# First attention: the norm of 512 tokens made alone, that of the other 1536 together; both batches prepared beside the first group's maxima; values cleared on ScalarE

## The chip, the cores and the metric

The kernel runs on one core of a Trainium2 chip. The metric is the device time of one execution in microseconds (us); lower is better. The profile is of one execution on that core, and its times count from the first instruction. Engines: TensorE (PE; its weight loads are PEld), VectorE (DVE), ScalarE (ACT), GpSimd (POOL) and SyncE (SP), which in this kernel issues the DMAs.

## The reference

Two layers of attention and experts over x of shape (2, 1024, 128), each `x = x + block(norm(x))`. The change lies in the first block:

```python
x = x + _L0_attn_ref(_layernorm(x, axis=-1), ...)

def _L0_attn_ref(x, ln_scale, ln_bias, wq, wk, wv):
    xn = _layernorm(x, ln_scale, ln_bias)
    q, k, v = (xn @ w, in 16 heads of 8, for w in wq, wk, wv)
    scores = einsum('bhid,bhjd->bhij', q, k)
    probs = softmax(scores / sqrt(128))
    return einsum('bhij,bhjd->bhid', probs, v) + xn
```

The outer norm and the norm inside the block are one norm in the kernel (L233 and L237), with scale and bias applied after the transposes. After this block come 8 experts (two chosen per token, and a shared one), a causal attention with 8 heads, and 16 experts.

## The kernel before, in words

The 2048 tokens are four chunks of 512 (`x_0` to `x_3`); two chunks are one batch item. Everything the change touches is in `attn0` and the helpers it calls.

Preparing a chunk has these pieces. `stats` (L129) takes mean and variance of four tiles of 128 tokens on VectorE. `rsqrt` (L117) makes the factors by Newton steps of small VectorE operations. L244 or L248 writes the normalised `xn`. TensorE transposes it (L167), scale and bias make `xT` (L270, L272 or, in `prep_x0`, a function that before never calls, L259 and L260), and `split` (L156) writes a rounded high part on ScalarE and the residual on VectorE or POOL (L159). `prep_k` and `prep_q` multiply by the weights in three passes (`mm3`, L163), split the result into two halves `hl0` and `hl1` (two buffers for each), store it in three DMAs of 256 KB (L304) into a scratch tensor in DRAM, and load it from there in the layout that the score matmuls want (`bands`, L308): 768 KB for k and q of the first group's chunks, 1 MB for others. The scratch tensors also hold rows of ones (L212, L221). `banded` (L294) makes the block of head group 0 directly, without DRAM. `prep_v` copies v into `V`, whose other columns are cleared at L224 and L225. `prep_res` (L328) adds the normalised x to the residual on POOL.

The attention itself runs over 16 groups n: a chunk of 512 queries and 4 heads each. For each group there are two streams. The score stream `s_unit` (L353) makes, for 128 queries, 512 keys and 2 heads, two matmuls (L363) and one VectorE maximum over them (L368): 16 units a group. After the last, `s_finish` (L376) writes the negated maxima into `mexp` (L379) and, four steps later, `row` makes `QX` (L387, L389, and L391 on ScalarE), the queries with the maximum as one more row. The second stream, `st_unit` (L398), makes transposed scores for 128 keys, one head and 512 queries (L407), ScalarE takes the exponential (L413), and `av_half` (L420) multiplies by V (L427): 32 units a group. `av_finish` and `av_add` (L439, L444) divide by the sum and add to x.

The order of TensorE is written out by hand (L506, `manual_schedule`); the order of the other engines and of the DMA queue is planned at build time by a simulated time line, with `issue_after` as fixed orders between two instructions of one engine, and is not changed at run time. A lead of 38 steps (L507) runs half a score unit a step, so 19 units, which are group 0 and three units of group 1. At step 1 and every fourth step it runs one piece of `side` (k of chunk 0, k of chunk 1, q of chunk 0, v of both) and some warming matmuls on ones (L374), whose result is not used. The main loop (L521) then runs one `st_unit` and half a score unit a step, so one group in 32 steps. There q of chunk 1 and the residuals come first, and from step 16 `prep((2, 3))` prepares the second batch item, one piece every fourth step, with two warming matmuls beside each between steps 16 and 54 (L532). The experts' weights of the first layer are loaded in the prologue (`ffn0_weights`, L219). Scores against QM and KS of other chunks are needed from group 4 (queries of chunk 1) and group 8 (second batch item).

Of the kernel before, what the change touches and what calls it, by code (L numbers as in the profile page):

```python
# [10 lines left out]
F32 = mybir.dt.float32  # L11
# [10 lines left out]
B = 2  # L22
# [50 lines left out]
class Net:  # L73
# [13 lines left out]
    def setup(self, ctx):  # L87
# [21 lines left out]
        nc.vector.memset(ones, 1.0)  # L109
        self.ones_r = self.const.tile([128, 128], F32R, name="ones_r")  # L110
# [6 lines left out]
    def rsqrt(self, v, n, name):  # L117
        nc = self.nc
        y = self.small.tile([128, n], F32, tag="rsy", name=f"rs_{name}")
        w = self.small.tile([128, n], F32, tag="rsw", name=f"rw_{name}")  # L120
# [8 lines left out]
    def stats(self, srcs, name):  # L129
        nc = self.nc  # L130
        n = len(srcs)
        st = self.small.tile([128, n, nc.vector.BN_STATS_DIM], F32, tag="bnst", name=f"bs_{name}", bufs=2)
# [23 lines left out]
    def split(self, dst, src, lo=None):  # L156
        nc = self.nc
        nc.scalar.copy(dst[0], src)  # L158
        (lo or nc.vector).tensor_sub(dst[1], src, dst[0].bitcast(F32))  # L159

# [8 lines left out]
    def attn0(self, ctx, cb, side_plan):  # L169
# [22 lines left out]
        ld = nc.sync.dma_start  # L192
        ld(out=wq0[0], in_=a["a0wq0"])
# [6 lines left out]
        ld(out=lnsb, in_=a["a0ln"].partition_broadcast(128))  # L200
# [10 lines left out]
        for c, k in list(scratch)[:3]:  # L211
            nc.sync.dma_start(out=scratch[c, k][:, :, 24:32, :], in_=self.hot_r.bitcast(F32))  # L212
        for x in mexp:
            nc.gpsimd.tensor_scalar_mul(x, self.ones.rearrange("p (t r) -> p t r", t=TPC), 0.0)
        nc.gpsimd.tensor_copy(id_r[0], self.ident)
        nc.gpsimd.tensor_scalar_mul(id_r[1], self.ident, hm[:, 4:5])
        self.load_x(2)
        self.load_x(3)
        self.ffn0_weights()  # L219
        for c, k in list(scratch)[3:]:  # L220
            nc.sync.dma_start(out=scratch[c, k][:, :, 24:32, :], in_=self.hot_r.bitcast(F32))  # L221
        for b in range(B):
            for i in range(2):
                nc.gpsimd.memset(V[b][i], 0.0)  # L224
                nc.gpsimd.memset(V[b][i][:, :, :, 8:9], 1.0)  # L225
        xns, xTs = {}, {}

        def prep_ln(cs, act=()):
            n = TPC * len(cs)
            src = [self.x[c][:, t, :] for c in cs for t in range(TPC)]  # L230
            mv = yield from self.stats(src, f"a0_{cs[0]}")
# [3 lines left out]
            if act:  # L235
                nm = self.small.tile([128, n], F32, tag="rsn", name=f"rn_a0_{cs[0]}")
                nc.vector.scalar_tensor_tensor(nm, mv[:, :, 0], -1.0, rs, ALU.mult, ALU.mult)  # L237
            yield
            for i, c in enumerate(cs):
                xn = xns[c] = self.tok.tile([128, TPC, D], F32, tag="xn", name=f"xn0_{c}")  # L240
                for t in range(TPC):
# [9 lines left out]
                    if t % 2 == 1:  # L251
                        yield
# [1027 lines left out]
```

## Time and profile before

| | us |
|---|---|
| three runs | 931.33, 937.6, 937.7 (median 937.6) |
| the profiled execution | 938.26 |
| its span, first to last instruction | 936.5 |
| first maximum of group 0 (L368) starts | 20.75 |
| last maximum of group 0 done (L379) | 45.76 |
| first transposed score (L407) | 48.06 |
| L379 of groups 1, 2, 3, 4, 5, 6 | 67.19, 93.89, 123.78, 144.30, 165.25, 184.81 |
| mean granted TensorE clock | 0.974 of full |

A row of the profile that ends in a bracket tells how long the engine was idle just before, and what released it. A row of the chain of waits is start, duration, and what ran; a row of a stage table is the stretch, its length, the busy time of PE, PEld, DVE, ACT and POOL with the number of instructions, the granted clock, the busy share of the 16 DMA engines and GB/s. A row of SyncE's waits has the total, the number and the longest.

### The profile page before, as it was taken

The page shows a single profiled execution, that of the slowest core. Times are in us where ns is not written, and L with a number is a line of the kernel's source. Part 1 is how long each engine was busy: PE and PEld are TensorE (multiplying, and loading weights), DVE is VectorE, ACT ScalarE, POOL GpSimd, SP SyncE. Part 2 cuts the span into 40 slices and gives each one's busy share as a digit, 9 for nine tenths or more (in the row PEclk, how much of TensorE's full clock was granted, in tenths as well). Part 3 has the DMA queues.
Part 4 walks back from the last instruction along what each step waited for, and adds up shares of the span by engine and source line. Part 5 has one row for each costly group of instructions (what it writes and reads, how often), then busy time and mean ns, then how long its engine had stood idle before and what let it go on. Part 6 is the DMA issues. An engine that isn't in the chain of part 4 may idle for free.

```text
span 936.5 us, 17186 instructions
## 1 busy us (share of the span) xinstructions
PE 889.5 (95%) x6469; PEld 602.9 (64%) x6469; DVE 800.3 (85%) x1636; ACT 597.9 (64%) x1153; POOL 315.7 (34%) x397
## 2 busy tenths in 40 slices
PE   7999899999999999989799998999999899998997
PEld 4543344444444443458688997988889799866775
DVE  7897789999999999358787788899979797799986
ACT  3178788998898898655344555445445355478775
POOL 9001300000010000023664757375737274236332
PEclk9999999999999999699999999999999999999999
DMA  6620440011000000023000001000000000064462
GB/s 181 203 79 1 149 145 1 1 46 57 13 27 10 1 1 2 2 95 100 13 9 4 12 21 49 1 24 1 2 2 24 2 25 12 24 192 152 143 199 70
DMA packets 32044, 49.13 MB, mean 52 GB/s; under 512 B 4544, under 2 KB 10488, under 8 KB 31960
## 3 DMA queue, kind: packets, MB, share of 16 engines
q1 hardware_dynamic: 31960, 48.03, 16.1%
q8 instruction: 51, 0.84, 0.4%
q14 instruction: 33, 0.27, 0.1%
HBM read 38.36 MB, written 9.65 MB: 51 GB/s over the span
## 4 chain that ended last, share of the span: by engine, by line
PE 66%; DVE 17%; ACT 7%; issue 5%; DMA 2%; POOL 1%; SPq 0%; DVEq 0%; ACTq 0%; POOLq 0%
PE av L427 14%; PE st L407 11%; PE o L905 10%; PE st L872 9%; ACT pt L413 3%; PE s L833 3%; DVE mx L368 2%; DVE f1f L1091 2%; PE vp L163 2%; PE hot L374 2%; PE qp L163 2%; PE st L879 2%; PE f0y L695 2%; DVE s L842 1%; PE stw L407 1%
## 5 line engine op out<-in xcount | busy, mean ns | idle before, releaser
L368 DVE TENSOR_REDUCE mx<-s 128x2 f32<-128x1024 f32 x256 | 299.7, 1219 | 21.6 <-PE s L363 18.3
L413 ACT ACTIVATE pt<-st 128x512 f32<-128x512 f32 x476 | 252.9, 602 | 32.7 <-PE s L363 21.2
L427 PE MATMUL av<-pt,V 128*32 128x256 f32 x2048 | 166.5, 405 | 0.0
L905 PE MATMUL o<-V,pt 128*128 128x129 f32 x1152 | 156.0, 276 | 1.5 <-ACT pt L884 0.7
L363 PE MATMUL s<-KS,QM 24*128 24x512 f32 x512 | 152.4, 499 | 3.0 <-DVE mx L368 2.1
L905 PEld LDWEIGHTS o<-V,pt 128*128 128x128 f32 x1152 | 148.7, 191 | 9.9 <-ACT pt L884 1.0
L407 PE MATMUL st<-QX,KS 25*128 25x512 f32 x476 | 144.8, 498 | 6.1 <-ACT pt L413 4.1
L872 PE MATMUL st<-Q,K 128*128 128x512 f32 (+1 forms) x480 | 136.6, 393 | 5.3 <-DVE rB_q L776 2.5
L407 PEld LDWEIGHTS st<-QX,KS 25*128 25x128 f32 x476 | 63.1, 182 | 101.4 <-ACT pt L413 47.2
L456 POOL TENSOR_TENSOR x<-x,ov 128x128 f32<-128x128 f32 x16 | 7.3, 454 | 322.4 <-DVE ov L453 322.4
L872 PEld LDWEIGHTS st<-Q,K 128*128 128x128 f32 x480 | 80.1, 191 | 16.9 <-DVE rB_q L776 3.7
L884 ACT ACTIVATE pt<-st 128x512 f32<-128x512 f32 x88 | 47.7, 544 | 59.6 <-PE st L879 51.8
L427 PEld LDWEIGHTS av<-pt,V 128*32 128x32 f32 x2048 | 42.9, 110 | 64.5 <-issue 61.1
L884 ACT ACTIVATE pt<-pt 128x512 f32<-128x512 f32 x72 | 43.2, 603 | 48.6 <-DVE pt L882 48.3
L363 PEld LDWEIGHTS s<-KS,QM 24*128 24x128 f32 x512 | 65.6, 183 | 11.4 <-DVE mx L368 7.9
L918 POOL TENSOR_TENSOR x<-x,w 128x128 f32<-128x128 f32 x128 | 59.3, 463 | 26.4 <-ACT w L916 22.0
L833 PE MATMUL s<-K,Q 128*128 128x512 f32 (+2 forms) x192 | 62.6, 357 | 0.8 <-DVE m L842 0.7
L163 PE MATMUL f1y<-f1s,f1w 128*128 128x512 f32 x192 | 56.3, 413 | 5.5 <-POOL f1s L159 3.1
L916 ACT ACTIVATE w<-o,rz 128x128 f32<-128x128 f32 x128 | 39.9, 364 | 33.4 <-DVE rz L912 29.0
L159 POOL TENSOR_TENSOR f1s<-f1f,f1s 128x512 fp32r<-128x512 f32 x24 | 36.2, 1510 | 59.6 <-ACT f1s L158 57.1
L1091 DVE SCALAR_TENSOR_TENSOR f1f<-f1f,f1gb 128x512 f32<-128x512 f32 x64 | 49.9, 797 | 7.4 <-ACT f1f L1090 6.6
L888 POOL TENSOR_SCALAR_AFFINE_SELECT pt<-pt 128x256 f32<-128x256 f32 x64 | 26.4, 415 | 86.8 <-ACT pt L884 86.6
(231 smaller groups left out, 1585.8 us busy)
## 6 DMA issues: line engine op xcount, KB each, us to landing
f1gb<-f1gd SPq DMA_DIRECT2D x64, 256.0 KB
f0gb<-f0gd SPq DMA_DIRECT2D x32, 128.0 KB
kd<-k SPq DMA_DIRECT2D x12, 256.0 KB
qd<-q SPq DMA_DIRECT2D x12, 256.0 KB
QM<-qd SPq DMA_DIRECT2D x3, 1024.0 KB
mb<-md SPq DMA_DIRECT2D x10, 256.0 KB
KS<-kd SPq DMA_DIRECT2D x2, 1024.0 KB
KS<-kd SPq DMA_DIRECT2D x2, 768.0 KB
```

The source lines that it names most:

```text
L163: self.nc.tensor.matmul(out, lhsT=lhs[l], rhs=rhs[r], start=start and i == 0, stop=stop and i == 2)
L363: self.last_s = nc.tensor.matmul(ps[:, k, :], lhsT=QM[c][r, g, cols(t)], rhs=KS[c // 2][r, g, cols(h, CH)], start=True, stop=True)
L368: self.marks["V"] = nc.vector.tensor_reduce(mxs[n][:, h, 2 * pr : 2 * pr + 2, t : t + 1], ps, AX.X, ALU.max, negate=True)
L407: nc.tensor.matmul(ps, lhsT=KS[c // 2][32 * j : 32 * j + 25, g, cols(kt)], rhs=QX[n][32 * j : 32 * j + 25, :], start=True, stop=True,)
L413: self.marks["A"] = nc.scalar.activation(e, ps, AF.Exp, scale=INV_SQRT_D)
L427: return nc.tensor.matmul(avs[n][cols(j, 32), q], lhsT=V[c // 2][kt // 4][:, kt % 4, 4 * g + j, :], rhs=es[j][:, q], start=kt == 0 and i = ...
L833: nc.tensor.matmul(s[:, 0 : k1 - k0], lhsT=Q[0][:, h, cols(qt)], rhs=K[0][:, k0:k1], start=True, stop=True)
L872: k = nc.tensor.matmul(o, lhsT=K[l][:, cols(kt)], rhs=Q[r][:, :, q0 : q0 + w], start=i == 0, stop=apart and i == 2)
L884: k = nc.scalar.activation(e[:, :, 256 - w :], o, AF.Exp, scale=INV_SQRT_D)
L905: nc.tensor.matmul(acc[t][:, h, :], lhsT=e[:, h, cols(t)], rhs=V[:, kt, h, :], start=(kt == 0 and h == 0), stop=(kt == qt and h == 1),)
L918: nc.gpsimd.tensor_add(xt, xt, w[:, h, :])
L1091: nc.vector.scalar_tensor_tensor(f, f, F7, gbs[e], ALU.min, ALU.mult)
```

## The change

Only chunk 0's norm is made ahead of the streams, by `prep_x0`; the statistics of chunks 1 to 3 go into VectorE's order behind chunk 0's `xn` and its split, and their factors are computed in one set of small operations of width 12 behind the first `banded` blocks. The lead's plan is a table by step: it now holds all of k, q and v of all four chunks, chunk 1's direct block at step 10, the last five rows of ones at step 5, and the residuals. The loads from DRAM (L308) are put off by three steps behind their stores, and are ordered on SyncE behind the last store issued so far. The order of group 0's score units becomes keys 0 to 511 for all queries, then keys 512 to 1023. In the main loop the second item's preparation and the warming matmuls of L532 go; the first experts' weights are loaded at step 24. `V` of the first item and `mexp` are cleared by ScalarE copies of a zero; `V` of the second item stays on POOL. x of chunks 2 and 3 is loaded ahead of the scratch rows. Two small buffers become single. The marks "L" and "D", which the cut diff mostly leaves out, name the last ScalarE piece and the last store, behind which later pieces are ordered.

```diff
+        self.zero = self.const.tile([128, 1], F32, name="zero")
+        nc.vector.memset(self.zero, 0.0)
...
-        w = self.small.tile([128, n], F32, tag="rsw", name=f"rw_{name}")
+        w = self.small.tile([128, n], F32, tag="rsw", name=f"rw_{name}", bufs=1)
...
-        st = self.small.tile([128, n, nc.vector.BN_STATS_DIM], F32, tag="bnst", name=f"bs_{name}", bufs=2)
+        st = self.small.tile([128, n, nc.vector.BN_STATS_DIM], F32, tag="bnst", name=f"bs_{name}", bufs=1)
...
-        ld(out=lnsb, in_=a["a0ln"].partition_broadcast(128))
+        self.load_x(2)
+        self.load_x(3)
...
-        for c, k in list(scratch)[:3]:
-            nc.sync.dma_start(out=scratch[c, k][:, :, 24:32, :], in_=self.hot_r.bitcast(F32))
+        def ones_rows(cks):
+            for c, k in cks:
+                nc.sync.dma_start(out=scratch[c, k][:, :, 24:32, :], in_=self.hot_r.bitcast(F32))
+            yield
+        run(ones_rows(list(scratch)[:3]))
+        ld(out=lnsb, in_=a["a0ln"].partition_broadcast(128))
+        for i in range(2):
+            nc.scalar.copy(V[0][i].rearrange("p k h e -> p (k h e)"), zero.to_broadcast([128, 2048]))
+            nc.gpsimd.memset(V[1][i], 0.0)
...
-            nc.gpsimd.tensor_scalar_mul(x, self.ones.rearrange("p (t r) -> p t r", t=TPC), 0.0)
+            nc.scalar.copy(x.rearrange("p t r -> p (t r)"), zero.to_broadcast([128, CH]))
+        for b in range(B):
+            for i in range(2):
+                nc.gpsimd.memset(V[b][i][:, :, :, 8:9], 1.0)
...
-        self.load_x(2)
-        self.load_x(3)
-        self.ffn0_weights()
-        for c, k in list(scratch)[3:]:
-            nc.sync.dma_start(out=scratch[c, k][:, :, 24:32, :], in_=self.hot_r.bitcast(F32))
-        for b in range(B):
-            for i in range(2):
-                nc.gpsimd.memset(V[b][i], 0.0)
-                nc.gpsimd.memset(V[b][i][:, :, :, 8:9], 1.0)
...
-        def prep_ln(cs, act=()):
+        after = {}
+        def behind(name):
+            return self.tc.issue_after(after[name].ins)
+        def ln_stats(cs):
...
-            mv = yield from self.stats(src, f"a0_{cs[0]}")
+            st = self.small.tile([128, n, nc.vector.BN_STATS_DIM], F32, tag="bnst", name=f"bs_a0_{cs[0]}", bufs=1)
+            mv = self.small.tile([128, n, 2], F32, tag="bnmv", name=f"mv_a0_{cs[0]}", bufs=2)
+            for i, c in enumerate(cs):
+                for t in range(TPC):
+                    k = i * TPC + t
+                    nc.vector.bn_stats(st[:, k, :], self.x[c][:, t, :])
+                    nc.vector.bn_aggr(mv[:, k, :], st[:, k, :])
+                yield mv
+        def ln_scale(cs, mv):
+            n = TPC * len(cs)
...
-            if act:
-                nm = self.small.tile([128, n], F32, tag="rsn", name=f"rn_a0_{cs[0]}")
-                nc.vector.scalar_tensor_tensor(nm, mv[:, :, 0], -1.0, rs, ALU.mult, ALU.mult)
-            yield
+            nm = self.small.tile([128, n], F32, tag="rsn", name=f"rn_a0_{cs[0]}", bufs=2)
+            nc.vector.scalar_tensor_tensor(nm, mv[:, :, 0], -1.0, rs, ALU.mult, ALU.mult)
...
-                xn = xns[c] = self.tok.tile([128, TPC, D], F32, tag="xn", name=f"xn0_{c}")
-                for t in range(TPC):
-                    k = i * TPC + t
-                    if c in act:
...
-                            xn[:, t, :], src[k], AF.Identity, bias=nm[:, k : k + 1], scale=rs[:, k : k + 1]
-                        )
-                    else:
-                        nc.vector.tensor_scalar(
-                            xn[:, t, :], src[k], mv[:, k, 0:1], rs[:, k : k + 1], ALU.subtract, ALU.mult
-                        )
-                    if t % 2 == 1:
-                        yield
+                lnp[c] = (mv, rs, nm, i * TPC)
+        lnp = {}
+        def prep_xn(c, act=range(TPC)):
+            mv, rs, nm, k = lnp[c]
+            xn = xns[c] = self.tok.tile([128, TPC, D], F32, tag="xn", name=f"xn0_{c}")
+            for t in range(TPC):
+                src = self.x[c][:, t, :]
+                j = slice(k + t, k + t + 1)
+                if t in act:
+                    self.marks["L"] = nc.scalar.activation(
+                        xn[:, t, :], src, AF.Identity, bias=nm[:, j], scale=rs[:, j]
+                    )
+                else:
+                    after["xn"] = nc.vector.tensor_scalar(xn[:, t, :], src, mv[:, k + t, 0:1], rs[:, j], ALU.subtract, ALU.mult)
+            yield
...
+            after["x"] = nc.vector.tensor_sub(xh[1], xT, xh[0].bitcast(F32))
...
-        def prep_x(c, dve=False, lo=None):
+        def prep_x(c, lo=None):
...
-            if dve:
-                nc.vector.tensor_scalar(xT, tp, lnT[:, 0:1], lnT[:, 1:2], ALU.mult, ALU.add)
-            else:
-                nc.scalar.activation(xT, tp, AF.Identity, bias=lnT[:, 1:2], scale=lnT[:, 0:1])
...
-                qload(c)
+                loads.append((self.u0, lambda: qload(c)))
...
+            after["b"] = nc.vector.tensor_sub(dst, p, t.bitcast(F32))
...
+                self.marks["D"] = nc.sync.dma_start(out=d[:, :, 8 * i : 8 * i + 8, :], in_=hl[w].bitcast(F32))
...
-            bands(KS[c // 2][:, :, cols(c % 2, CH)], store(hl, (0, 1, 0), c, 1), 1 if c < 2 else 0)
-            yield
...
+            d = store(hl, (0, 1, 0), c, 1)
+            loads.append((self.u0, lambda: bands(KS[c // 2][:, :, cols(c % 2, CH)], d, 1 if c < 2 else 0)))
+            yield
+        loads = []
...
-        def prep(cs):
-            yield from prep_ln(cs, cs)
-            for c in cs:
-                yield from prep_x(c, lo=nc.gpsimd)
-            for c in cs:
-                yield from prep_k(c)
-            for c in cs:
-                yield from prep_q(c)
-            for c in cs:
-                yield from prep_v(c)
-                yield from prep_res(c)
+        def prep_b(c, w, k, dst):
+            banded(dst, w, c, k)
+            yield
+        def weights0():
+            with self.tc.issue_after(self.marks["D"].ins):
+                self.ffn0_weights()
+            yield
...
+        s_stream[:16] = [(0, t, h, pr) for h in range(2) for t in range(TPC) for pr in range(2)]
...
-        W0 = 22
...
-        NW = 6
...
-        for _ in range(W0):
-            nc.tensor.matmul(hot, lhsT=self.ones_r, rhs=self.hot_r, start=True, stop=True)
-        run(prep_ln((0, 1), act=(1,)))
-        run(prep_x(0), prep_x(1, True))
+        dense(hot, 14)
+        for mv in ln_stats((0,)):
+            ln_scale((0,), mv)
+        run(prep_xn(0, (1, 3)))
+        st123 = ln_stats((1, 2, 3))
+        with behind("xn"):
+            next(st123)
+        run(prep_x0(0))
+        with behind("x"):
+            next(st123)
+            mv = next(st123)
+        dense(hot, 6)
...
-        for c in range(2):
-            banded(KS[0][:, 0, cols(c, CH)], wk0, c, 1)
+        banded(KS[0][:, 0, cols(0, CH)], wk0, 0, 1)
+        dense(hot, 5)
+        with behind("b"), self.tc.issue_after(self.marks["L"].ins):
+            ln_scale((1, 2, 3), mv)
+            run(prep_xn(1), prep_res(0))
+        x1, x2, x3 = (prep_x(c, nc.gpsimd) for c in (1, 2, 3))
+        lead = {
+            1: (prep_k(0),),
+            3: (prep_q(0),),
+            5: (x1, ones_rows(list(scratch)[3:])),
+            7: (x1, prep_v(0), prep_res(1)),
+            9: (prep_xn(2),),
+            10: (prep_b(1, wk0, 1, KS[0][:, 0, cols(1, CH)]),),
+            12: (prep_k(1),),
+            14: (prep_v(1),),
+            16: (x2,),
+            17: (prep_xn(3),),
+            18: (x2, prep_res(2)),
+            20: (prep_k(2),),
+            22: (x3,),
+            24: (x3, prep_q(1), prep_res(3)),
+            26: (prep_k(3),),
+            28: (prep_q(2),),
+            30: (prep_q(3),),
+            32: (prep_v(2),),
+            34: (prep_v(3),),
+        }
...
-        for g in (prep_k(0), prep_k(1), prep_q(0), prep_v(0), prep_v(1)):
-            side.add(g)
...
-                if u % 4 == 3 or u == 1:
-                    warm(3 if side.q else NW)
-                    side.step()
+                self.u0 = u
+                for g in lead.get(u, ()):
+                    side.add(islice(g, 1))
+                    side.drain()
+                while loads and loads[0][0] + 3 <= u:
+                    with self.tc.issue_after(self.marks["D"].ins):
+                        loads.pop(0)[1]()
+                if u % 2 == 1:
+                    warm(2 if u in lead else 3)
...
-            side.drain()
-            for g in (prep_q(1), prep_res(0), prep_res(1)):
-                side.add(g)
...
-            plan = {16: lambda: prep((2, 3))}
-            plan.update(side_plan)
+            plan = {24: weights0, **side_plan}
...
-                    if 16 < u < 54:
-                        dense(self.pt([128, CH], f"hot_{u}"), 2)
...
```

## The prediction

> **What bounds the kernel now.** I read the page first, then the stage table of the first attention, then VectorE's timeline, then SyncE's waits. From the page:
>
> ```profile
> span 936.5 us, 17186 instructions
> PE 889.5 (95%) x6469; PEld 602.9 (64%) x6469; DVE 800.3 (85%) x1636; ACT 597.9 (64%) x1153; POOL 315.7 (34%) x397
> L368 DVE TENSOR_REDUCE mx<-s 128x2 f32<-128x1024 f32 x256 | 299.7, 1219 | 21.6 <-PE s L363 18.3
> ```
>
> The 256 maxima of L368 (16 for each of 16 groups) are VectorE's largest item, and 18.3 us of its idle time before them waits for score matmuls. The shares hide where; the stages show it (TensorE, its weight loads, VectorE, ScalarE, POOL, then granted clock, DMA share, GB/s):
>
> ```profile
> 20.00:48.00 28.00, 25.92 (x112) 16.05 (x112) 23.94 (x24) 3.62 (x7) 4.18 (x4) 0.94 0.53 169
> 48.00:80.00 32.00, 31.77 (x270) 14.13 (x270) 29.90 (x52) 24.70 (x47) 0.00 (x0) 1.00 0.17 59
> 80.00:144.00 64.00, 59.59 (x542) 26.64 (x540) 51.00 (x54) 51.95 (x102) 11.51 (x11) 0.95 0.33 108
> 164.00:184.00 20.00, 19.93 (x211) 8.28 (x203) 19.51 (x20) 18.29 (x36) 0.45 (x1) 1.00 0.01 2
> ```
>
> From 164 on VectorE is busy 19.51 of 20 us: it sets the pace. From 80 to 144 it is busy 51 of 64. There the second batch is prepared beside both streams. VectorE's timeline dates the groups, since L379 follows a group's last maximum:
>
> ```profile
> 45.76 0.18 DVE L379 TENSOR_TENSOR mexp<-mx 128x16 fp32r<-128x16 f32 x1
> ...
> 116.12 0.69 DVE L159 TENSOR_TENSOR q<-pq,q 128x512 fp32r<-128x512 f32 x1 [2.32 <-ACT q L158]
> ...
> 123.78 0.19 DVE L379 TENSOR_TENSOR mexp<-mx 128x16 fp32r<-128x16 f32 x1
> ...
> 165.25 0.19 DVE L379 TENSOR_TENSOR mexp<-mx 128x16 fp32r<-128x16 f32 x1
> ...
> 184.81 0.19 DVE L379 TENSOR_TENSOR mexp<-mx 128x16 fp32r<-128x16 f32 x1
> ```
>
> Groups 0 to 6 end at 45.76, 67.19, 93.89, 123.78, 144.30, 165.25 and 184.81. So groups 1 to 5 take 21.43, 26.70, 29.89, 20.52, 20.95, in sum 119.49; group 6 takes 19.56 and the next two 19.5. Five groups at 19.5 are 97.5: the preparation costs the main loop 22.0 us. The chain of waits and SyncE's waits name the worst stop:
>
> ```profile
> 106.89 0.69 DVE k L159
> ...
> 108.84 6.51 DMA kd<-k
> ...
> 115.51 0.58 ACT q L158
> ```
>
> ```profile
> SPq L308 <- DMA kd<-k: 7.3, 5, 3.3
> SPq L308 <- DMA qd<-q: 5.4, 3, 3.0
> ```
>
> The last q of the batch cannot be split until k's stores have left its buffer (two buffers per half), and on SyncE stores queue behind loads that wait for earlier stores to land. k's split ended at 106.85, its stores landed at 115.35: 8.5 us.
>
> **The sum.** It is made on the profiled execution: 938.26 us, span 936.5, 0.66 above the median 937.6. Everything after group 5 is taken as unchanged, so the new time is 938.26 plus (new end of group 5 minus 165.25).
>
> **Prologue.** Before, the first maximum starts at 20.75. With 512 tokens alone: x is there at 3.85; four statistics with their aggregates are half of the eight from 3.85 to 6.04, 1.1; 13 small operations of L233 to L237 at 0.20 are 2.6 (in before they take 5.39, as 1.74, 0.63, 0.54 and 0.53 stand among them while POOL clears V and mexp), so the factors stand between 7.6 and 10.0. From the first xn (11.46) to the first score matmul (19.97) before takes 8.5. The change saves there L272's pass before the split (0.6), the second K block (one L298 of 0.85 on ScalarE) and chunk 1 in VectorE's order (0.3): 6.7. First maximum at 7.6 + 6.7 + 0.7 = 15.0; ends 15.0 and 17.4. I take 15.5, near the quick end, because mexp's clearing (two of 1.47 on POOL) is gone. ScalarE's clearing: 128 columns cost 0.30 and 512 cost 0.58, so 2048 are about 1.7; two of these and two of 0.58 make 4.6. They go into ScalarE's idle 2.93 before 5.01 and 4.54 before 11.57, so I cost them at nothing; if one stands just ahead of xn it costs up to 1.7. The warming matmuls (14, 6, 5 for 22) run while PE waits for the others: nothing, or 0.8 if the six outlast the first split. x of the second half is loaded ahead of the scratch rows; SyncE's five later ones and the FFN weights move into the loop, out of a queue that nothing waits for there. The later single small buffers are used by VectorE alone, in its own order: nothing.
>
> **First group on VectorE.** 16 maxima at 1.16 (seven take 8.19) are 18.6; 13 small operations for three chunks 2.5; chunk 1's block 0.6; four k and four q residuals at 0.6, since the next starts 0.09 early, 4.8: together 26.5 (before, 25.0 with 4.6 of waits). TensorE's order is by hand, so chunk 1's transposes hold all behind them until its norm is there. In the main loop of before the small operations took 7.4 (73.16 to 80.54) in the gaps between maxima. Here some fit ahead of the first maximum: ready about 6 after it, plus 1.65 for xn on ScalarE, 23.2 against 20.8 in a free run: 2.4 lost. Without the DMA, group 0 ends at 15.5 + 26.5 + 2.4 = 44.4.
>
> **The queue.** SyncE now has, before the last q may be split: stores of k0, q0, k1, k2, q1, k3 (0.786 MB each), five scratch rows (1.31 MB) and the loads of k0, q0, k1 (0.786 each) and k2 (1.05). Stores run at 313 GB/s, loads at 391:
>
> ```profile
> 24.00:26.00 2.00, 1.91 (x9) 1.20 (x9) 1.99 (x3) 0.58 (x1) 0.18 (x1) 1.00 1.01 313
> 128.00:130.00 2.00, 2.00 (x24) 0.72 (x24) 2.00 (x3) 1.89 (x5) 0.00 (x0) 1.00 1.03 391
> ```
>
> That is 15.1 + 4.2 + 8.7 = 28.0 us from about 19 on: with no gap k3's stores land at 47. A gap opens where a load on SyncE waits for its stores while later stores stand behind it; two such waits as the longest of before (3.3 and 3.0) make it 53.3. Halfway, 50; then 0.6 of split and 1.4 on VectorE: group 0 ends at 52.0 (ends 44.4, where the DMA never holds, and 55.3). TensorE, ScalarE's QX and the maxima all wait behind that split.
>
> **The skill's rule for the queue.** The trace shows 391 GB/s for a load. The Trainium skill, "DMA: Bandwidth & Descriptors", section "Where 436 GB/s comes from", gives about 358 for a core's HBM transfers; the measured window is above it. By its figure the same 9.4 MB take 26 us, an estimate, against 28.0, and the sum would be some 2 us lower.
>
> **Groups 1 to 5.** Removed from them: statistics and small operations (3.1 + 2.2), four residuals (2.4), 3.3 + 2.8 + 3.5 of ScalarE, the stop of 2.32 and the 18 filler matmuls of L532. Left: the ten fillers of L536 in group 1, q2's and q3's late loads (needed at groups 4 and 8), and at step 24 six loads, one cast of 0.66 that may wait for its DMA, and 1.88 on POOL. I take 20.5, 20.0, 20.0, 19.6, 20.0 = 100.1; ends 97.5 (all steady) and 108.5 (half of the 22.0 stays). What comes late next is VectorE itself.
>
> **Sum.** Group 5 ends at 52.0 + 100.1 = 152.1, 13.1 earlier: 925.1, and 0.66 less against the median: about 924.5.
>
> **A rule against the change.** Row: with no filler the window 164 to 184 has clock 1.00, while in before the clock falls to 0.50 at 36 to 38 and 118 to 120, with fillers. The Trainium skill, "TensorE: Matmul & The Clock Gate", section "Part 1: The HAM clock gate", halves the clock after an idle window of about 3.4 us. If each of groups 1 to 4 fell into one such window at half clock, that would add up to 4 x 1.7 = 7 us, an estimate: 931.5 in place of 924.5.
>
> **The rivals.**
> 1. The queue keeps up (for: DMA share is only 0.53 from 20 to 48; against: the waits of 3.3 and 3.0 there). Group 0 ends at 44.4, time 938.26 + 144.5 - 165.25 = 917.5, less 0.66: 917.
> 2. The cost comes back: half of the excess stays in groups 1 to 5 (108.5) and the queue's late end holds (55.3). Group 5 ends at 163.8: 936.8, or 936 against the median. For it: group 5 of before has no preparation and still takes 20.95, with 1.21 of wait for TensorE. Against: groups 6 to 8 run at 19.5.
> 3. Slower: the two buffers and SyncE's order become the bound of the lead. Each buffer is used four times, so the last q's split comes three rounds after the first use of its buffer, at about 18, and group 0 ends 2 later. One round is a split of 0.6 and the time to landing. At the 8.5 of before group 0 ends at 18 + 27.3 + 2 = 47.3, within the sum. At 14.4 it ends at 65, which is break-even; from 17.6 on (74.6) the kernel is slower by over 1%; at 20 group 0 ends at 81.8: 938.26 + 81.8 + 100.1 - 165.25 = 954.9, or 954. For: twice the traffic of before's second batch stands in one queue, with the scratch rows in it. Against: the volume alone ends at 47.
>
> **How the numbers follow.** The forecast has 0.45, rival 1 0.13, rival 2 0.22, rival 3 0.20. A measurement of this kernel can tell about 1% from no change, so faster (below 928) is forecast and rival 1, 0.58; rival 2 is the same, 0.22; rival 3 slower, 0.20. The forecast's own range is 917 to 930 (group 0 between 46 and 55.3, groups 1 to 5 in 98 to 102). For 8 in 10 the range goes from 914, below rival 1, to 946, past rival 2 and into the first part of rival 3.
>
> **What would show it.** Right: the first maximum near 15.5; the last q's residual on VectorE behind a wait for ScalarE, that behind a DMA of k, near 50; group 0's L379 near 52; L379 to L379 at 19.5 to 20.5 from then on. Wrong: maxima of groups 1 to 4 that wait for TensorE, a granted clock under 0.9 in them, or a lead that ends after 65 (65.15 + 100.1 = 165.25 is the break-even).

## The result, and the profile after

The changed kernel takes 967.11 us (median of six runs, 955.76 to 970.75) against 936.67 for the kernel before on the same chip (median of six, 931.33 to 957.24): a ratio of 1.0283, interval 1.0223 to 1.0343. It is slower, by about 2.8%, where about 924.5 was forecast. Here and below a ratio leaves disturbed executions out and a median does not, so the one need not be the quotient of the other. The profiled execution took 966.86, its span 965.1; the mean granted clock of its span is 0.937, that of before 0.974.

From the page of the changed kernel (L388 is the maximum, L368 before; L383 the score matmul, L363 before):

```profile
span 965.1 us, 17171 instructions
PE 922.5 (96%) x6463; PEld 616.9 (64%) x6463; DVE 798.9 (83%) x1634; ACT 603.4 (63%) x1159; POOL 310.2 (32%) x394
PEclk7855999999999697989999999999999899999999
L388 DVE TENSOR_REDUCE mx<-s 128x2 f32<-128x1024 f32 x256 | 300.4, 1220 | 60.5 <-PE s L383 55.2
```

VectorE has the same work (798.9 us against 800.3). What grew is its wait for score matmuls ahead of the maxima, 55.2 us against 18.3, and TensorE's busy time, by 33 us for six matmuls fewer. The clock's row says why that can be: slices 2 to 4 (24 to 97 us) have 0.8, 0.5 and 0.5.

The stage table of the changed kernel (TensorE, its weight loads, VectorE, ScalarE, POOL, then granted clock, DMA share, GB/s):

```profile
20.00:48.00 28.00, 25.98 (x84) 14.37 (x82) 15.23 (x21) 11.29 (x23) 10.06 (x8) 0.79 0.65 216
48.00:80.00 32.00, 32.00 (x69) 17.07 (x68) 11.65 (x13) 5.12 (x9) 5.01 (x4) 0.51 0.71 222
80.00:100.00 20.00, 20.00 (x92) 10.28 (x92) 10.91 (x10) 8.35 (x16) 0.00 (x0) 0.59 0.18 59
120.00:140.00 20.00, 19.91 (x213) 8.38 (x205) 19.47 (x20) 18.31 (x36) 0.45 (x1) 1.00 0.01 2
```

From 48 to 80 TensorE is busy all of 32 us, with 69 matmuls (270 in before), at a clock of 0.51, while VectorE works 11.65 us (29.90 in before). From 120 on VectorE sets the pace again, 19.47 of 20: what was forecast for groups 1 to 5. By the clock in stretches of 1 us, TensorE has half its clock from 14 to 31 and from 49 to 96; in before only from 15 to 19, 36 to 39, 87 to 90 and 118 to 121 in this part.

VectorE's timeline of the changed kernel (start, duration; L399 closes a group of maxima, as L379 before):

```profile
19.49 1.22 DVE L388 TENSOR_REDUCE mx<-s 128x2 f32<-128x1024 f32 x1
...
65.38 1.23 DVE L388 TENSOR_REDUCE mx<-s 128x2 f32<-128x1024 f32 x1 [2.78 <-PE s L383]
69.98 1.23 DVE L388 TENSOR_REDUCE mx<-s 128x2 f32<-128x1024 f32 x1 [3.38 <-PE s L383]
71.12 0.68 DVE L161 TENSOR_TENSOR q<-pq,q 128x512 fp32r<-128x512 f32 x1
71.72 0.17 DVE L399 TENSOR_TENSOR mexp<-mx 128x16 fp32r<-128x16 f32 x1
...
106.90 0.19 DVE L399 TENSOR_TENSOR mexp<-mx 128x16 fp32r<-128x16 f32 x1
...
126.97 0.18 DVE L399 TENSOR_TENSOR mexp<-mx 128x16 fp32r<-128x16 f32 x1
```

| stretch | before | forecast | after | after less forecast |
|---|---|---|---|---|
| first maximum starts | 20.75 | 15.5 | 19.49 | +4.0 |
| from it to the end of group 0 | 25.0 | 36.5 | 52.2 | +15.7 |
| group 1 | 21.4 | 20.5 | 35.2 | +14.7 |
| groups 2 to 5 | 98.1 | 79.6 | 81.4 | +1.8 |
| the rest of the span | 771.3 | 771.3 | 776.8 | +5.6 |

The last column adds up to 41.8: the profiled execution against the forecast's 925.1. Groups 2 to 5 give back 16.7 us of before, where 18.5 was forecast; groups 0 and 1 cost 41 more than in before. In the last row the changed kernel has long stretches at half clock at 318 to 335 and 366 to 380, and before one at 381 to 398; that these make the 5.6 was not tested.

What the lead looks like on TensorE in the changed kernel, at full clock and at half (start, duration; two steps of the lead are one unit of VectorE's maxima):

```profile
32.34 0.49 PE L383 MATMUL s<-KS,QM 24*128 24x512 f32 x1
32.76 0.97 PE L166 MATMUL pb<-xT,wk0s 128*128 128x512 f32 x3
33.66 0.49 PE L383 MATMUL s<-KS,QM 24*128 24x512 f32 x1
34.07 0.97 PE L394 MATMUL hot<-hot_r,ones_r 128*128 128x512 f32 x3
34.97 0.50 PE L383 MATMUL s<-KS,QM 24*128 24x512 f32 x1
...
62.25 0.79 PE L383 MATMUL s<-KS,QM 24*128 24x512 f32 x1
62.97 1.65 PE L166 MATMUL pq<-xT,wq 128*128 128x512 f32 x3
64.55 0.79 PE L383 MATMUL s<-KS,QM 24*128 24x512 f32 x1
65.27 1.65 PE L394 MATMUL hot<-hot_r,ones_r 128*128 128x512 f32 x3
66.85 0.79 PE L383 MATMUL s<-KS,QM 24*128 24x512 f32 x1
```

From one even step's score matmul to the next there are 2.63 us at full clock (34.97 - 32.34) and 4.60 at half (66.85 - 62.25), with no gap. VectorE needs 26.5 / 16 = 1.66 us for a unit, by the forecast's list. So TensorE bounds such units even at full clock, and the maxima wait for it 38.2 us between 18 and 100:

```profile
DVE mx L388 <- PE s L383: 38.2, 20, 3.7
```

SyncE's waits in the changed kernel, against 7.3 for kd before; none of them reaches the split of the last q, which never waits for a DMA here:

```profile
SPq L328 <- DMA kd<-k: 6.8, 3, 3.9
```

### The profile page after: what moved, and what is told of

It reads as the page before. It is cut to its first block, busy times and chain, and to the rows that moved or that the text cites. A ratio compares the mean times of both kernels' runs of the same rounds, so it can differ in the third digit from the quotient of the medians.

```text
span 965.1 us, 17171 instructions
## 1 busy us (share of the span) xinstructions
PE 922.5 (96%) x6463; PEld 616.9 (64%) x6463; DVE 798.9 (83%) x1634; ACT 603.4 (63%) x1159; POOL 310.2 (32%) x394
## 3 DMA queue, kind: packets, MB, share of 16 engines
q1 hardware_dynamic: 31960, 48.03, 15.5%
## 4 chain that ended last, share of the span: by engine, by line
PE 68%; DVE 16%; ACT 7%; issue 5%; POOL 1%; DMA 1%; SPq 0%; DVEq 0%; ACTq 0%; POOLq 0%
PE av L447 14%; PE st L427 11%; PE o L956 10%; PE st L923 9%; PE hot L394 4%; ACT pt L433 3%; PE s L884 3%; PE s L383 2%; DVE f1f L1142 2%; PE qp L166 2%; PE vp L166 2%; PE st L930 2%; PE f0y L746 1%; DVE mx L388 1%; DVE s L893 1%
## 5 line engine op out<-in xcount | busy, mean ns | idle before, releaser
L388 DVE TENSOR_REDUCE mx<-s 128x2 f32<-128x1024 f32 x256 | 300.4, 1220 | 60.5 <-PE s L383 55.2
L383 PE MATMUL s<-KS,QM 24*128 24x512 f32 x512 | 168.3, 533 | 1.8 <-DVE KS L319 1.6
L447 PE MATMUL av<-pt,V 128*32 128x256 f32 x2048 | 169.0, 410 | 0.0
L427 PE MATMUL st<-QX,KS 25*128 25x512 f32 x476 | 148.8, 520 | 2.1 <-DVE a1wvo L161 0.6
L935 ACT ACTIVATE pt<-st 128x512 f32<-128x512 f32 x88 | 47.7, 544 | 61.6 <-PE st L930 53.7
L383 PEld LDWEIGHTS s<-KS,QM 24*128 24x128 f32 x512 | 70.5, 195 | 20.2 <-issue 9.3
L967 ACT ACTIVATE w<-o,rz 128x128 f32<-128x128 f32 x128 | 39.9, 364 | 33.3 <-DVE rz L963 28.9
L161 POOL TENSOR_TENSOR f1s<-f1f,f1s 128x512 fp32r<-128x512 f32 x24 | 36.8, 1534 | 59.0 <-ACT f1s L160 56.5
L939 POOL TENSOR_SCALAR_AFFINE_SELECT pt<-pt 128x256 f32<-128x256 f32 x64 | 26.5, 416 | 88.5 <-ACT pt L935 88.4
```

The costliest lines, as they stand in the source:

```text
L383: self.last_s = nc.tensor.matmul(ps[:, k, :], lhsT=QM[c][r, g, cols(t)], rhs=KS[c // 2][r, g, cols(h, CH)], start=True, stop=True)
L388: self.marks["V"] = nc.vector.tensor_reduce(mxs[n][:, h, 2 * pr : 2 * pr + 2, t : t + 1], ps, AX.X, ALU.max, negate=True)
L427: nc.tensor.matmul(ps, lhsT=KS[c // 2][32 * j : 32 * j + 25, g, cols(kt)], rhs=QX[n][32 * j : 32 * j + 25, :], start=True, stop=True,)
L447: return nc.tensor.matmul(avs[n][cols(j, 32), q], lhsT=V[c // 2][kt // 4][:, kt % 4, 4 * g + j, :], rhs=es[j][:, q], start=kt == 0 and i = ...
L935: k = nc.scalar.activation(e[:, :, 256 - w :], o, AF.Exp, scale=INV_SQRT_D)
```

## The experiments

The theory after the result (**density**): the clock follows how dense TensorE's work on all 128 rows is. In the lead, pieces listed at even steps come between the two 24-row score matmuls of a unit, so these run one at a time; the stream is then thin enough that a clock once halved does not come back, and the lead is TensorE's, at half clock. Rivals: a **stall** (TensorE's wait of 1.92 us for POOL at 44.9 closes the clock and is the cause); the **prologue** (its first stretch at half clock, 14 to 31); and **VectorE or the queue**, as forecast. Ratios are to the kernel before on the same chip (936.8 to 942.4 us there), with intervals of 95%.

**The pairs kept together, e5_pairs.** The even steps' pieces move to the odd steps, where the pair is done; 51 warming matmuls as before.

```diff
-            12: (prep_k(1),),
-            14: (prep_v(1),),
+            13: (prep_k(1),),
+            15: (prep_v(1),),
...
-            34: (prep_v(3),),
+            35: (prep_v(3),),
...
-                    warm(2 if u in lead else 3)
+                    warm(2 if u in (1, 3, 5, 7, 9, 17) else 3)
```

> The changed kernel with the lead's pieces of even steps moved one step later, to odd ones, the number of warming matmuls per odd step kept. In the changed kernel a piece at an even step stands between the two score matmuls of a unit (24 rows each, two row groups), so they run one after the other, 0.42 us each at full clock and 0.72 at half, instead of together. Density theory: 14 pairs run together again, which saves 5 us at full clock and 10 at half, and the share of full-array work rises from about two thirds to 80 per cent; the gate closes later or reopens sooner; time 935 to 955. If the split pairs matter only by their length: the half-clock stretch stays to the end of the lead, 953 to 960. If they do not matter: 960 to 970.

Measured: 934.7 (median of ten), ratio 0.9946 (0.9903 to 0.999). Group 0 ends at 60.26, groups 1 to 5 take 20.4, 20.1, 19.4, 20.9, 20.9. Half clock from 16 to 30 and 44 to 47. The unit, then the stages, of e5_pairs:

```profile
30.57 0.49 PE L383 MATMUL s<-KS,QM 24*128 24x512 f32 x2
30.99 0.97 PE L166 MATMUL pb<-xT,wk0s 128*128 128x512 f32 x3
31.80 0.85 PE L394 MATMUL hot<-hot_r,ones_r 128*128 128x512 f32 x3
32.57 0.50 PE L383 MATMUL s<-KS,QM 24*128 24x512 f32 x2
```

```profile
20.00:48.00 28.00, 25.37 (x92) 15.18 (x92) 17.10 (x21) 12.25 (x24) 10.81 (x9) 0.76 0.74 236
48.00:80.00 32.00, 31.10 (x219) 16.79 (x217) 25.19 (x25) 18.12 (x34) 4.30 (x4) 1.00 0.70 241
```

Two score matmuls side by side take 0.49, as one alone did; the unit is 2.00 us (32.57 - 30.57) in place of 2.63. From 48 to 80 the clock is 1.00 and not 0.51, and 219 matmuls run in place of 69. This one edit, of order only, takes 32 us off the median (3.4% by the two ratios). It is not a chance of one profile: the mean clock is 0.932 to 0.949 in all six runs of the changed kernel and 0.965 to 0.981 in the seven runs of e5 that its ratio uses (0.939 to 0.946 in its other three, at 952 to 959 us). Between the two profiles 26 us lie in groups 0 and 1 (group 1 ends at 80.7 and not at 106.9). What was hidden now shows, in the chain of e5_pairs:

```profile
49.83 0.54 DVE q L161
...
50.43 0.59 DVE mx L388
51.03 6.27 DMA qd<-q
...
57.39 0.69 DVE q L161
```

The last q's split waits for an earlier q's store (4.2 us on ScalarE): the queue that the prediction named, some 7 us later, and behind a store of q where it named one of k.

**The same with fewer warming matmuls, e12_pairs_thin.** It separates density from amount: 32 matmuls fewer (6431 against 6463).

```diff
-                    warm(2 if u in (1, 3, 5, 7, 9, 17) else 3)
+                    warm(1)
```

> The run with pairs together and one warming matmul per odd step instead of two or three: 26 fewer in the lead. Density theory: the share of full-array work in the lead falls again, the gate closes for most of the lead, group 0 ends at 65 or later and the time is 938 to 960. If the pairs mattered by their length alone: 26 times 0.23 us off TensorE, 928 to 934.

Measured: 959.35, ratio 1.0245 (1.0198 to 1.0291); the clock at half from 17 to 81, in one piece. The stages of e12_pairs_thin:

```profile
20.00:48.00 28.00, 26.07 (x73) 14.85 (x71) 16.36 (x21) 11.38 (x23) 10.04 (x8) 0.50 0.57 189
48.00:80.00 32.00, 32.00 (x96) 17.89 (x94) 17.73 (x18) 10.83 (x19) 5.03 (x4) 0.50 0.85 282
```

Less work on TensorE, and 2.5% slower than before; the mean clock is 0.923 to 0.933 in all four runs. Group 0 still ends at 62.14, since its unit takes 2.73 us at half clock; group 1 takes 28.9, and the profile has half clock again at 303 to 317 and 368 to 413.

**More of them, e2_warm6, e14_warm4, e18_pairs_pool_order_warm4.** e2 puts six in the changed kernel's odd steps without a piece (`warm(2 if u in lead else 6)`). e14 is e5 with `warm(4)`, with the loads of the last two k and one residual listed later (e9 and e10 below); e18 is e17 (below) with `warm(4)`.

> The changed kernel with six warming matmuls instead of three on the lead's odd steps without a piece: 39 more, some 9 us of TensorE at full clock. Clock theory: blocks of six reopen the gate as they do in the kernel before at 36 to 40, so the half-clock stretch from 48 to 96 shrinks to a few us; time 940 to 955 in spite of the added work. If the clock is not the cause, the added work comes on top: 972 to 985.

> The run with pairs together, residual and loads late, and four warming matmuls on every odd step (33 more). If the gate's second closing (at 43) is what is left: it stays open from the first reopening on, group 0 ends at 52 to 56, 926 to 932. If the added work costs more than the clock returns: 33 times 0.23 us is 7.6 us, group 0 ends at 60 or later, 936 to 945.

> The same with four warming matmuls a step. If TensorE is the bound of a lead at full clock: no waits of TensorE over 1 us, a step pair of 2.2 us, group 0 ends at 54 to 57 and not earlier, 927 to 935, with the clock at 1.00 from 30 on. If not: group 0 at 52 or earlier.

Measured: e2 962.79 (942.98 to 965.7; no interval), group 0 only at 82.28; half clock 14 to 38 and 52 to 79. This profile is of the longest of its four runs; in the shortest the mean clock was 0.979, so e2 does not decide. e14 944.9, ratio 0.9975 (0.9916 to 1.0034); e18 935.6, ratio 0.9941 (0.9864 to 1.0018), group 0 at 60.56. The stages of e14_warm4, and its unit:

```profile
20.00:48.00 28.00, 26.04 (x116) 16.46 (x115) 18.43 (x25) 12.90 (x25) 11.75 (x10) 0.97 0.68 228
48.00:80.00 32.00, 32.00 (x223) 17.76 (x222) 25.35 (x25) 17.67 (x33) 3.43 (x3) 1.00 0.76 248
```

```profile
32.41 0.49 PE L383 MATMUL s<-KS,QM 24*128 24x512 f32 x2
32.84 0.96 PE L166 MATMUL pk<-xT,wk 128*128 128x512 f32 x3
33.64 1.09 PE L394 MATMUL hot<-hot_r,ones_r 128*128 128x512 f32 x4
34.66 0.49 PE L383 MATMUL s<-KS,QM 24*128 24x512 f32 x2
```

With the clock open from 22 on (0.97, 1.00) group 0 still ends at 56.9: units of 2.25 us, 16 of them 36. What holds the clock open is itself the lead's length. With two to four warming matmuls a unit TensorE bounds this lead either way: even at e5's 2.00 us, 16 units from its first maximum at 18.34 end at 50.3, an estimate, so the forecast's 44.4 without the queue was not to be had.

**The stall, e1_res_late and e16_pool_order.** At 44.9 TensorE waits 1.92 us for POOL, which does a residual ahead of the low half of x; the row is of the changed kernel. e1 lists that residual at the last step that has a piece; e16 orders it behind that half on POOL itself.

```profile
46.85 0.73 PE L166 MATMUL pk<-xT,wk 128*128 128x512 f32 x2 [1.92 <-POOL xT L161]
```

```diff
# e1
-            18: (x2, prep_res(2)),
+            18: (x2,),
...
-            34: (prep_v(3),),
+            34: (prep_v(3), prep_res(2)),
# e16
+            with self.tc.issue_after(self.last_lo.ins):
                 nc.gpsimd.tensor_mul(xn, xn, lnsb[:, 0:1, :].to_broadcast([128, TPC, D]))
```

> The changed kernel with the residual of chunk 2 moved from step 18 to step 34 of the lead, so that POOL makes the low half of chunk 2's x before it, and TensorE does not wait 1.92 us for it at 44.4. Clock theory: that wait is what closes TensorE's clock gate at 48.2, and the lead then runs at half clock until 96.5. Without the wait the gate stays open there, group 0 ends near 58 instead of 71.7, and the time is 940 to 950. Density theory: the lead's stream itself (a third of it score matmuls on 24 rows) cannot hold the gate open; it closes a few us later all the same, and the time stays within 960 to 970. Queue theory (the prediction's): the last q waits for k's stores; the clock is no matter, and the time stays within 960 to 970 with a DMA wait in ScalarE's idle time.

> The changed kernel with only POOL's order fixed: the residual of a chunk is made after the low half of its x, so TensorE's wait of 1.92 us at 44.4 goes or shrinks below 1 us. Stall theory: without the wait the gate stays open, group 0 ends near 58 and the time is 940 to 950. Density theory: the pairs are still split and the gate closes within a few us all the same; half clock to the end of the lead, 957 to 968.

Measured: e1 961.83, ratio 1.0275 (1.0205 to 1.0345). It tested nothing: POOL's timeline of e1 has the residual where it was, ahead of L161, and TensorE still waits 1.94.

```profile
41.09 1.27 POOL L355 TENSOR_TENSOR x<-x,xn 128x512 f32<-128x512 f32 x1
42.31 1.26 POOL L161 TENSOR_TENSOR xT<-xT,xT 128x512 fp32r<-128x512 f32 x1
```

e16 took the wait away: 969.17, ratio 1.03 (1.022 to 1.0381). The stage table of e16_pool_order over one long stretch:

```profile
17.00:106.00 89.00, 89.00 (x222) 47.28 (x222) 37.74 (x48) 23.02 (x44) 15.54 (x13) 0.50 0.50 161
```

TensorE is busy all of the 89 us, the stall is gone, and the clock is at half throughout. So the time is lost without the stall too, and a busy TensorE is not enough for the clock. Why it opened at 31 in the changed kernel and not here stays open.

e16 does not clear the stall of closing an open clock, since here the clock was at half from 17 on. The other traces speak for that part. In twelve kernels the clock was open ahead of this wait (0.85 us in e18, 1.42 to 1.94 in the changed kernel, e1, e2, e4, e5, e6, e9, e10, e11, e13 and e15) and fell to half within 2 us of the wait's end; in e14 (1.93) and e17 (0.85) it stayed open. What the order changes is how long it then stays at half: 47, 55 and 48 us with the pairs split (the changed kernel, e1, e4), 3 to 17 with them together. That the wait starts the stretch is read from these traces; no run takes the wait away whole while the clock is open.

**The prologue, e4_fill_in_place.** In the changed kernel all 25 fillers of the prologue ran in one row from 3.15 to 11.25, ahead of the transposes, since the planner of the order placed them; e4 fixes the last eleven behind the work they follow in the text.

```diff
-        dense(hot, 6)
+        with self.tc.issue_after(self.last_pe.ins):
+            dense(hot, 6)
```

> The changed kernel with the prologue's warming matmuls held in their written places (14, then 6 after the transposes, then 5 after the first blocks); in the changed kernel all 25 run ahead of the transposes. Clock theory: the first half-clock stretch, 14.7 to 31.7, goes or shortens, the transposes come 1.1 us earlier, group 0 ends 4 to 9 us earlier, but the second stretch stays: 957 to 963. If the planner's place of them does not matter: 965 to 969.

Measured: 958.55, ratio 1.0237 (1.0173 to 1.0301). The first maximum comes at 17.51, 2 us earlier, and the first stretch shrinks to 22 to 29. The second stays (46 to 94), and with it group 0 at 69.25 and group 1 at 35.5. The prologue is not the cause of the second stretch; that it costs time of its own is not shown, since the intervals of e4 and of the changed kernel (1.0223 to 1.0343) overlap.

**The kernel before, e3_before_thin, e7_before_split, e8_before_nofill.** Is before itself held by density? e3 takes warming matmuls away (`NW = 2` for 6), e7 moves preparation and warming between the two halves of a pair (`u % 4 == 2 or u == 0`), e8 leaves out the 18 fillers of L532.

> The kernel before with two warming matmuls instead of six in the lead's steps without a piece. Clock theory: after the dip at 35 to 40 the gate does not reopen in the lead; half clock from about 36 to the burst of five near 55; 3 to 10 us slower than before. If fillers only cost time: 16 to 20 matmuls of 0.23 us less, 1 to 4 us faster.

> The kernel before with its lead's pieces and warming matmuls at even steps, so that they stand between the two score matmuls of a unit. Density theory: ten pairs run apart, 0.35 us each at full clock, and the gate stays closed longer after 36: 4 to 15 us slower than before. If the place in the pair is no matter: within 2 us of before.

> The kernel before without the 18 warming matmuls of the main loop (steps 18 to 50), which the change also takes out. If they hold the clock there: the gate closes in groups 1 to 3 for 10 us or more, 3 to 15 us slower. If they only fill: 18 times 0.23 us, up to 4 us faster, or within 2 us since VectorE and the DMA set the pace there.

Measured: e3 951.04, ratio 1.014 (1.007 to 1.0211), with half clock from 36 to 60 where before has 36 to 39; group 0 ends earlier, at 42.95, and groups 1 to 3 take 29.1, 28.2, 31.3 (21.4, 26.7, 29.9 in before). e7 963.92, ratio 1.0199 (1.0103 to 1.0294), half clock 14 to 28, 35 to 42, 45 to 62 and 66 to 72, group 0 at 64.82; but this profile is of the longest of its four runs (973.7), and TensorE there also waits for the maxima (eight times, up to 1.31), so e7 alone would not decide. e8 942.81, ratio 1.0053 (1.0011 to 1.0095), no long stretch in groups 1 to 4: those fillers do little.

**Variants on the pairs: e9_pairs_loads_late, e10_pairs_res_late, e11_pairs_res_loads, e17_pairs_pool_order.** e9 puts the loads of the last two k, and of the q listed between them, off to step 36 (`self.u0 if c < 2 else 33`, and the three steps of the change), out of the way of the stores; e10 lists e1's residual late in e5; e11 does both; e17 is e9 with e16's order on POOL.

> The run with pairs together, and the loads of chunk 2's and 3's k and chunk 1's q put off to the end of the lead, so that on SyncE no store stands behind a load that waits. Queue theory (the prediction's third step): with the clock held, q's split waited 4.2 us for a store of q; this goes, group 0 ends 3 to 5 us earlier than 60.3, the time falls by 3 to 5 us against the run with pairs (934.7), to about 930. If that wait is hidden by something else in the lead: no change, 932 to 937.

> The run with pairs together, and the residual of chunk 2 on POOL moved to the end of the lead, so that TensorE does not wait 1.93 us for the low half of chunk 2's x. Stall theory: group 0 ends 3 to 5 us earlier (the wait, and the dip of the clock after it), 929 to 932. If the queue behind it takes the gain back (the next q then waits longer for its buffer): within 1 us of 934.7, with a DMA wait on ScalarE of 7 us or more instead of 4.2.

> Both: the residual of chunk 2 late and the loads late. If stall and queue are two stops in a row: group 0 ends near 52 (where the prediction had it), 925 to 929, 1 per cent below the kernel before. If one covers the other: 930 to 934.

> Pairs together, loads of the later chunks late, and POOL's order fixed. If the stop was worth its length and the dip after it: group 0 ends at 52 to 56, 925 to 932. If TensorE's work bounds the lead: group 0 at 56 to 60 and 930 to 938.

Measured: e9 947.91 (937.35 to 967.81, four runs, no interval); q's wait for a DMA falls from 4.2 to 1.8, but the half clock lasts from 17 to 44 and from 51 to 58, and group 0 ends at 64.84: undecided as to time. e10 947.7, ratio 1.0031 (0.9977 to 1.0086): POOL's order again did not change, so e10 is e5 run again. The gain over the changed kernel repeats (ratio 1.0031 against 1.0283); e5's gain over before does not. e11 935.03, ratio 0.9965 (0.9923 to 1.0007), group 0 at 57.23. e17 933.88, ratio 0.995 (0.988 to 1.0021), group 0 at 62.14 after half clock from 16 to 47.

**With the prologue's fillers fixed: e6_pairs_fill, e13_fill, e15_fill_warm4.** e4 on top of e5, e11 and e14.

> The same, and the prologue's warming matmuls held in their written places. Density theory: adds the 3 to 8 us of the first half-clock stretch: 930 to 950, group 0 ends between 48 and 60. If the two do not add: as the run with pairs alone.

> The run with pairs together, residual and loads late, and the prologue's warming matmuls held in their written places. If the first half-clock stretch is what is left of the lead's excess: the first maximum starts near 17.6 instead of 19.4, the clock is at half for 7 us at most before 31, group 0 ends at 50 to 54, and the time is 922 to 930. If it is not: group 0 at 56 or later and 932 to 938.

> Both of these. If each closes one stretch at half clock: full clock from 30 on at the latest, group 0 ends at 50 to 55, 922 to 930. If TensorE's own work is then the bound of the lead: 930 to 938 with a clock of 1.00 in the lead.

Measured: ratios 0.9991 (0.9946 to 1.0036), 1.0016 (0.9972 to 1.0061), 0.9994 (0.9944 to 1.0043). In e6 and e13 the first maximum comes at 17.66 and 17.64, but the time does not follow: the first microseconds were not what decided, and the profiles of e6 and e15 have half clock later (303 to 320; 377 to 404).

**All leads side by side.** The share is 128-row matmuls in a unit's time, from the chain of waits of each kernel; the stretch is the longest at half clock up to the end of group 1, each read from the one profiled run of its kernel.

| lead | unit, us | share | longest stretch, us |
|---|---|---|---|
| split, 2 or 3 warming (after, e1, e4, e16) | 4.60 at half | 3.16 / 4.60 = 69% | 47, 55, 48, 89 |
| pairs, 1 (e12) | 2.73 at half | 2.01 / 2.73 = 74% | 64 |
| split, 6 (e2) | 5.88 at half | 4.44 / 5.88 = 76% | 27 |
| pairs, 3 (e5, e6, e9, e10, e11, e13, e17) | 2.00 | 1.58 / 2.00 = 79% | 14, 7, 27, 17, 10, 17, 31 |
| pairs, 4 (e14, e15, e18) | 2.25 | 1.82 / 2.25 = 81% | 7, 3, 14 |

The order of the rows is that of the density theory; the spread within a row says that the share alone is no exact switch, and the row of e2 rests on the longest of its four runs.

## Why the prediction was wrong

**The step that failed is "First group on VectorE".** It costed the lead by VectorE's list alone (26.5 us and 2.4) and gave TensorE's side no sum. The rows for one stood in before's trace: the lead lists about a k, q, v or transpose piece in each unit, and three warming matmuls. At the changed kernel's own full-clock durations a unit is 2.63 us, 16 of them 42.1, against 28.9 for VectorE. By this estimate group 0 would have ended at 57.6 from the forecast's first maximum, and at 61.6 from the measured one, even with an open clock, instead of 44.4. What is left to 71.72 is mostly the clock: 34 us of group 0's maxima (19.5 to 31, 49 to 71.7) and 24 of group 1 ran at half. e5, e12 and e14 show both parts: order alone takes the unit from 2.63 to 2.00, and density alone (e5 to e12) puts 64 us at half clock.

**"A rule against the change" looked in the wrong place.** It put the clock's risk at four windows of 1.7 us in groups 1 to 4 and named their granted clock as the sign. The stretch was 47 us long, began in the lead and ran through most of group 1, +14.7 there. The row is e16's: busy 89.00 of 89.00 us at a clock of 0.50. The Trainium skill, "TensorE: Matmul & The Clock Gate", section "Part 1: The HAM clock gate", has the clock doubled after about 3.4 us of sustained activity. Read as busy time of the profile, that does not agree with e16, where these 89 us did not open it, so the measurement decides: busy time in the profile is not enough. The Trainium skill, "Perfetto Trace Analysis", section "Matmul Optimizations", asks for matmuls back to back in batches because power follows utilisation. Back to back alone did not do it here, since e16 had no gap in its 89 us at half clock; e5, with the same matmuls in another order, had 14 us at half clock where the changed kernel had 47.

**"Prologue" was mis-sized by 4.0.** The first maximum came at 19.49, past the 15.5 that was taken and past the late end's 17.4. Shown in part: with the fillers in place it comes at 17.39 to 17.66 (e4, e6, e13, e15), and at 18.32 to 20.13 in the other variants of the changed kernel, so the "nothing" for the warming matmuls was 0.7 to 2.7. The rest is read from the timeline, not tested: VectorE sits idle 1.93 us until ScalarE's pass over the same transposed tile is done, and the statistics of chunks 2 and 3 stand ahead of the first block. ScalarE's clearing cost nothing, as forecast: V's two took 3.69, mexp 1.13, ahead of xn.

**"The queue" did not come to the test.** In the changed kernel no wait of ScalarE is put down to a DMA between 18 and 100; that its slow lead gave the stores the time is argued, not shown. With the pairs together (e5) such a stop is there, behind a store of q, 4.2 us before the split at 57, where 50 was forecast.

**"Groups 1 to 5" came out for 2 to 5** (81.4 against 79.6: 20.1, 19.5, 19.4, and 22.3 for group 5, in which the clock falls at 175 to 178). Group 1 failed for the lead's reason. "After group 5 unchanged" missed by 5.6, where the late stretches at half clock differ; they differ from kernel to kernel, and why is open.

**Rival 3 had the sign and the place** (group 0 ends after 65; it ended at 71.7) by luck, for its mechanism was wrong: no wait for the two buffers or for a DMA held the lead. The "wrong" sign that the prediction named, maxima of groups 1 to 4 that wait for TensorE and a clock under 0.9, was seen in group 1.

**What can be had.** The arrangements with pairs together and at least two warming matmuls a unit have ratios between 0.9941 and 1.0031 (e9 has none), within 1% of the kernel before. The 13 us forecast do not come: the lead's TensorE work, the warming beside it and the stops that are left end group 0 between 56.9 and 62.2 (64.8 and 65.0 in e9 and e10) and not at 52. What stays open: by what measure the clock is granted, whether the wait for POOL starts the second stretch, and what sets the late stretches.

## What to carry to other kernels

When work is moved into a stage, sum it on every engine, the one that "only waits" above all: here TensorE's 42 us stood behind VectorE's 29 and nobody had added them up. Small matmuls that run side by side must stay adjacent in the order written by hand; a piece between them costs their time twice (0.42 us each in place of 0.42 for both) and leaves a smaller share of 128-row work. Read the granted clock stage by stage with the busy share beside it: in e16 a stage was 100% busy at 0.50, and in e12 and e3 taking filler away made the kernel slower.

## What the runs showed that was not expected

- The clock stayed at half for 47 to 89 us with TensorE busy without a gap (the changed kernel, e16), and at 79 to 81% of 128-row work it came back 3 to 17 us after it fell at the wait for POOL (44 to 47 in e5, 45 to 62 in e10, the same order).
- Two 24-row score matmuls that stand side by side take as long as one (0.49 us in the timeline at full clock, 0.79 at half).
- Listing an operation at a later step did not move it on POOL (e1, e10), and 25 fillers written in three places ran as one row (the changed kernel); only an explicit order did (e4, e16).
